# X W of all strips made after the scores, from x1^T kept in att's memory, with VectorE's order in the sort and the fillers moved

## Chip, cores and metric

One core of a Trainium2 chip runs the whole program in one launch. The metric is device time in microseconds (us) of that core. Three runs of the kernel before gave 740.38, 743.62 and 736.76, median 740.38.

## What is computed

N = 2708 nodes with D = 128 features x, and a 0/1 matrix adj (N x N), all float32. Two layers; the change lies where the first ends and the second begins.

```python
# layer 0
deg = clip(adj.sum(1), 1); dis = deg ** -0.5
diffusion = (dis[:, None] * adj * dis[None, :]) @ x - x
attn = softmax(beta * cos_sim(x, x) * adj, axis=1)
x1 = layernorm(x + diffusion + sigmoid(alpha) * (attn @ x - x))
# layer 1
XW = x1 @ W
s_col, s_row = XW @ a[:D], XW @ a[D:]
den = exp(leaky_relu(s_row[:, None] + s_col[None, :], 0.01))
num = adj @ den
att = where(num != 0, den / num, 0)
out = layernorm(x1 + adj @ (att @ XW))
```

## The kernel before

`den` splits into products of exponentials on either side of the bend of leaky_relu. The kernel sorts the nodes by s_row (the k side) and s_col (the j side) into 24 groups of at most 126, and for each group needs one gathered block of rows of adj^T and one of X W. Rows are held in 22 blocks of 128; columns of adj^T in 6 strips of 512 (the last of 148).

**Attention** (up to about 215 us): `att` [128 x 22 x 128] collects the attention term of all blocks. It lies in the pool `lp`, which is closed at L950, before the sort.

**Diffusion** (L865 to L946). For each strip, 22 matmuls `dif_acc` (each written as two instructions), turning, the layer norm into `x1`, turning of x1 (`x1_ps`), and `x1_in_sbuf` (L807), which copies x1^T to `x1_t`. From it come two rows of scores (`scores`, L815: `row` with k = 1 and `col` with k = 0), tallies of how many scores lie below each of 256 thresholds (`tally`, L666), `shared_row` (L832, on ScalarE), and `picked` (L823, scores by node: `sr_p`, `sc_p`). `limited` and `e2` (L839 to L846) make `low` and exp of it, `e2_p`, and put it into `e2_w`. Then `projected` (L848) makes four blocks of X W on TensorE, VectorE copies them to `xw`, and `store_xw` (L857) stores them to the tensor `xw_d` in HBM on ScalarE's queue. Strips 0 to 3 do all this in a loop that Tile orders; strips 4 and 5 (`s` and `t`, from L894) follow in an order that is written out by hand: while `strict` is set, the helpers `mm`, `dve`, `act` and `gps` (L181 to L201) pin each instruction behind the last one of its engine. All their instructions carry the lines of these helpers in the profile (L176 to L201).

**Fillers.** One more sum over all rows of adj^T, weighted by `e2_w`, is kept in two PSUM banks (`tot`). Its work is cut in 22 jobs "e" (`first_strips`, L691: loads a 768 KB row block into `nat`, a pool of three buffers, and 4 matmuls, each two instructions) and 22 jobs "k" (`kept_strips`, L707: 6 matmuls from strips 3, 4 and 5, which are in SBUF). The first nine e jobs load on GpSimd's queue during the diffusion. The rest are placed by hand: `fill("eke")` issues three jobs at that point of TensorE's order; their loads go on SyncE's queue, each waiting for its buffer.

**The look-up of intervals' ends** (`reached`, L737; L984 to L996). From the tallies a table `reach_b` [128 x 256] says where an interval that begins at each threshold ends. Eleven steps on VectorE follow it, each needing the one before (L988): `ends[g] = reach_b[ends[g-1]]`. The result `both` goes through two rounds of matmuls (`ends_ps`, `thr_ps`) to the thresholds `thr`.

**The sort** (L968 to L1242). VectorE: `k_gt`, `k_hot`, a scan `k_run`, `k_own` (which needs `ahead` from TensorE), `k_at`, `k_onp`; then the same for j. ScalarE writes `k_ons` and `j_ons` block by block (`valued`). TensorE makes tables from `onp` and `ons` (`table`, L1101), with fillers between a table and the choice of its rows (`k_sel`). `k_no` (L1116) holds row numbers: with it GpSimd gathers 126 rows of adj^T into `ring` (four buffers; ring 0 is `x_sb`'s memory, the others lie where the strips were), and with `j_no` rows of `xw_d` into `xws`.

**The main loop** (L1340): 24 groups through `num`, `q` and `m_acc`; then the output matmuls.

Pools are stacks at both ends of SBUF. `tab` and `tmp` (L963, L965) are opened at the right end after `lp`, `work2` and `nat` of the diffusion were closed or as they become free, so their tiles lie over old tiles. With `reuse_waits="tile"` the first write to a new tile waits for every reader and writer of each old tile that it overlaps, DMAs among them.

Of the kernel before, what the change touches and what calls it, by code (L numbers as in the profile page):

```python
# [9 lines left out]
F32 = mybir.dt.float32  # L10
AF = mybir.ActivationFunctionType
ALU = mybir.AluOpType
# [33 lines left out]
def grouped(  # L46
# [16 lines left out]
    def pool(name, bufs=1, space=None, side="left", stack=ctx):  # L63
        kw = {"space": space} if space else {}
        return stack.enter_context(
            tc.tile_pool(name=name, bufs=bufs, side=side, reuse_waits="tile", **kw)
        )
# [7 lines left out]
    def blocks(s):  # L75
        return min(SW // P, NB - s * (SW // P))
# [110 lines left out]
    def dve(op, *args, **kwargs):  # L187
        if strict:
            return pinned("DVE", getattr(nc.vector, op), *args, **kwargs)
        return getattr(nc.vector, op)(*args, **kwargs)  # L190

    def act(op, *args, **kwargs):
        if strict:
            return pinned("ACT", getattr(nc.scalar, op), *args, **kwargs)
        return getattr(nc.scalar, op)(*args, **kwargs)  # L195
# [450 lines left out]
    strip_a = pool("strip_a", stack=l0)  # L646
    strip_b = pool("strip_b", stack=l0)
    strip_c = pool("strip_c", stack=l0)
    nat = pool("nat", 3, stack=l0)
    work2 = pool("work2", 2, stack=es)  # L650
    tots = ExitStack()
    ps_tot = pool("ps_tot", 1, PSUM, side="right", stack=tots)
# [63 lines left out]
    def fill(pattern):  # L716

        for c in pattern:
            f, kb = jobs[c].pop(0)
            f(kb, nc.sync)  # L720
# [84 lines left out]
        return tp  # L805

    def x1_in_sbuf(s, tp):  # L807
        nb = blocks(s)
        x1_t = work2.tile([P, SW], F32, tag="x1_t", name="x1_t")
        dve(  # L810
            "tensor_copy", x1_t[:, : nb * P], tp[:, :nb, :].rearrange("p b i -> p (b i)")
        )
        return x1_t

    def scores(s, x1_t, k, pb):  # L815
# [7 lines left out]
    def picked(s, pb, dst):  # L823
        for b in range(blocks(s)):
            ib = s * 4 + b
            junk = work2.tile([P, P], F32, tag="picked", name="picked", bufs=2)
            dve(
                "scalar_tensor_tensor", junk, pb[:, ts(b, P)], 1.0, ident, ALU.mult,
                ALU.mult, accum_out=dst[:, ib : ib + 1],
            )  # L830

    def shared_row(s, pb):  # L832
        n = blocks(s) * P
        act(
            "activation", sr_b[:, s * SW : s * SW + n], pb[:, :n], AF.Copy,
            scale=1.0 - LEAK,
        )

    def limited(b0, b1):  # L839
        dve(  # L840
            "tensor_scalar", low[:, b0:b1], sr_p[:, b0:b1], LIMIT, -LIMIT, ALU.min, ALU.max
        )

    def e2(b0, b1):
        act("activation", e2_p[:, b0:b1], low[:, b0:b1], AF.Exp, scale=LEAK)
        nc.gpsimd.tensor_copy(e2_w[:, b0:b1, 1], e2_p[:, b0:b1])  # L846

    def projected(s, x1_t):  # L848
        pn = ps_mm.tile([P, SW // P, D], F32, tag="mm", name="xw_ps")
        for b in range(blocks(s)):  # L850
            mm(
                nc.tensor.matmul, pn[:, b, :], x1_t[:, ts(b, P)], w_sb,
                start=True, stop=True,
            )
        return pn

    def store_xw(s, xw, nb):  # L857
        nc.scalar.dma_start(
            xw_d[s * SW : s * SW + nb * P, :].rearrange("(b p) d -> p b d", p=P), xw
        )  # L860

    def score_bank():
# [2 lines left out]
    for s in range(NS - 2):  # L865
        v, nb = width(s), blocks(s)
        if s > 0:
            load_strip(s + 1)
        acc = ps_acc.tile([P, SW], F32, tag="acc", name="dif_acc")
        diffuse(s, acc)  # L870
        if s == 0:
            attended(*ended)
        h = mixed(s, turned(to_sbuf(acc, v, nb), nb, ps_tp))
        to_x1(s, h, *moments(h, nb))
        x1_t = x1_in_sbuf(s, x1_turned(s))
        pbs = []
        for k in (1, 0):
            pb = scores(s, x1_t, k, score_bank())
            tally(s, pb, k)
            pbs.append(pb)  # L880
        shared_row(s, pbs[0])
        picked(s, pbs[0], sr_p)
        picked(s, pbs[1], sc_p)
        limited(s * 4, s * 4 + nb)
        e2(s * 4, s * 4 + nb)
        xw = work2.tile([P, 4, D], F32, tag="xw", name="xw")
        nc.vector.tensor_copy(xw, projected(s, x1_t))
        store_xw(s, xw, nb)

        for kb in {1: (0, 1, 2), 2: (3, 4, 5), 3: (6, 7, 8)}.get(s, ()):  # L890
            first_strips(kb, nc.gpsimd)
# [18 lines left out]
    tally(s, row_s, 1, (0,))  # L910
    h_t = mixed(t, rows)
    mv_t = moments(h_t, blocks(t))
    shared_row(s, row_s)
    fill("eke")
    tally(s, row_s, 1, (1,))
    to_x1(t, h_t, *mv_t)
    tp = x1_turned(t)
# [12 lines left out]
    far = small.tile([P, 2], F32, tag="far", name="far")  # L930
    dve("tensor_scalar", far, ct[:, 2:4], G + 0.5, None, ALU.add)
    shared_row(t, row_t)
    picked(t, col_t, sc_p)
    picked(t, row_t, sr_p)
    picked(s, row_s, sr_p)
    fill("ek")
    reach_ps, can = reached(ct_ps)
    limited(s * 4, NB)
    picked(s, col_s, sc_p)
    act("activation", reach_b[64:], can[64:], AF.Copy, scale=-1.0, bias=Q + 1.0)  # L940
    dve("tensor_copy", reach_b[:64], reach_ps[:64, :Q])
    e2(s * 4, NB)
    xw = nat.tile([P, 6, D], F32, tag="xw_last", name="xw", bufs=1)
    act("copy", xw[:, :4, :], projected(s, x1_s))
    act("copy", xw[:, 4:, :], projected(t, x1_t)[:, :2, :])
    store_xw(s, xw, 6)  # L946
    fill("ekekek")
    es.close()
    pss.close()
    lps.close()  # L950
# [14 lines left out]
    tmp = pool("tmp", side="right", stack=sort)  # L965
    ps_x = pool("ps_x", 2, PSUM, stack=sort)

    vk = tmp.tile([P, NB], F32, name="vk")  # L968
    dve("scalar_tensor_tensor", vk, sr_p, -1.0, pad, ALU.mult, ALU.add)
    vj = tmp.tile([P, NB], F32, name="vj")  # L970
    dve("tensor_tensor", vj, sc_p, pad, ALU.add)
    back = tab.tile([P, NB], F32, name="back")
    dve("tensor_tensor", back, live, e2_p, ALU.mult)


    ons = {}
# [8 lines left out]
    ends = tmp.tile([P, half_g], F32, name="ends")  # L985
    dve("tensor_copy", ends[:64, 0:1], reach_b[:64, 0:1])
    dve("tensor_copy", ends[64:, 0:1], reach_b[64:, Q - 1 :])
    for g in range(1, half_g):  # L988
        junk = tmp.tile([P, Q], F32, tag="more", name="junk")
        dve(  # L990
            "scalar_tensor_tensor", junk, bound_no, ends[:, g - 1 : g], reach_b,
            ALU.is_equal, ALU.mult, accum_out=ends[:, g : g + 1],
        )
    both = tmp.tile([P, NG - 1], F32, name="both")
    dve("tensor_scalar", both[:, : half_g - 1], ends[:, : half_g - 1], row0, None, ALU.mult)
    dve("tensor_scalar", both[:, half_g - 1 :], ends, half_on, None, ALU.mult)  # L996
    ends_ps = ps_x.tile([P, SW], F32, tag="ahead", name="ends_ps", bufs=2)
    mm(nc.tensor.matmul, ends_ps[:, : NG - 1], ones, both, start=True, stop=True)
    thr_ps = ps_x.tile([P, SW], F32, tag="x", name="thr_ps", bufs=2)
    fill("k")  # L1000
    for h in range(2):
# [5 lines left out]
        mm(  # L1007
            nc.tensor.matmul, thr_ps[:, : NG - 1], ones, hit, start=(h == 0), stop=(h == 1)
        )
    fill("ekekk")  # L1010
    thr = tmp.tile([P, NG + 1], F32, name="thr")
    gps("memset", thr[:, 0:1], -1e9)
    gps("memset", thr[:, NG:], 100.0)
# [19 lines left out]
    def numbered(name, hot):  # L1033

        run = tmp.tile([P, NG, NB], F32, tag=name + "_gt", name=name + "_run")
        dve(
            "tensor_tensor_scan",
            run.rearrange("p g b -> p (g b)"), going.rearrange("p g b -> p (g b)"),
            hot.rearrange("p g b -> p (g b)"), 0.0, ALU.mult, ALU.add,
        )  # L1040
        of = tab.tile([P, NG], F32, name=name + "_of")
        dve("tensor_copy", of, run[:, :, NB - 1])
        ahead = ps_x.tile([P, SW], F32, tag="ahead", name="ahead", bufs=2)
        mm(nc.tensor.matmul, ahead[:, :NG], after, of, start=True, stop=True)
        return run, ahead, of
# [54 lines left out]

    def table(name, onp, v, o, p0, between):  # L1101

        t = tmp.tile([P, 1, P], F32, name=f"{name}_t{v}")
        partial_table(name, onp, v, o)
        act("copy", t[:, 0, :], o)
        between()
        return selected(name, t, [v], p0)

    def banks(*tags):
        return [  # L1110
            ps_x.tile([P, SW], F32, tag=tag, name="tab_ps", bufs=2)[:, :P] for tag in tags
        ]
# [26 lines left out]
            oob_is_err=False,  # L1139
        )  # L1140


    cs_p = tmp.tile([P, NB], F32, name="cs_p")
    dve("tensor_scalar", cs_p, sc_p, LIMIT, -LIMIT, ALU.min, ALU.max)
    dve("tensor_scalar", cs_p, cs_p, 1.0 - LEAK, None, ALU.mult)

    k_gt = beyond("k", vk)
    k_hot = grouped_by("k", k_gt)
    k_run, k_ahead, k_of = numbered("k", k_hot)
    valued("k", 0, k_hot, from_n)  # L1150
    valued("k", 1, k_hot, low, 0, 17)
    fill("kekekekek")
    j_gt = beyond("j", vj)
    k_own = chosen("k", k_hot, k_run, k_ahead)
    k_onp = placed("k", k_own)
    j_hot = grouped_by("j", j_gt)
    k_tab = table("k", k_onp, 0, *banks("x"), P - G, lambda: fill("kk"))
    valued("k", 1, k_hot, low, 17)
    valued("j", 1, j_hot, cs_p, 0, 12)
    j_run, j_ahead, j_of = numbered("j", j_hot)  # L1160
    k_no = rows_of_table("k", k_tab, G)
    valued_by_dve("j", 0, j_hot, from_n)
    k_tab = table("k", k_onp, 1, *banks("x"), 0, lambda: fill("kkk"))
    valued("j", 1, j_hot, cs_p, 12)
    fill("k")
    assert not any(jobs.values()), jobs
    j_own = chosen("j", j_hot, j_run, j_ahead)

# [745 lines left out]
```

## Time and profile before

| what | value |
| --- | --- |
| median of 3 runs | 740.38 us (736.76 to 743.62) |
| the profiled execution: time, span | 739.68 us, 737.9 us |
| TensorE busy in the span | 708.7 us, 96% |
| VectorE, ScalarE, GpSimd busy | 443.8, 419.5, 233.9 us |
| mean granted TensorE clock | 0.982 |
| diffusion | about 217 to 345 us |
| tallies, look-up, sort | about 345 to 395 us |
| main loop from | 395.3 us |

How to read it: times count from the start of the profiled span. PE is TensorE's matmuls and PEld its weight loads, DVE VectorE, ACT ScalarE, POOL GpSimd, SP SyncE; a "q" behind a name means that the engine's queue issued a DMA. In the timeline a row gives start, length, engine, line, operation, tiles written and read, shape and count; at its end, in brackets, the idle time of that engine before it and what ended it. Neighbours of one kind are merged and may overlap others. A view of waits gives who waited for whom, us in total, times, longest.

### The profile page before, as it was taken

To read this page: it belongs to the slowest core of one execution; us is meant where nothing else is said; L and a number is where in the kernel's file an instruction comes from. 1 tells how busy PE (TensorE), PEld (TensorE's weight loads), DVE (VectorE), ACT (ScalarE), POOL (GpSimd) and SP (SyncE) were. 2 spreads that over 40 slices of the span, in tenths; PEclk is the share of its full clock that TensorE was granted. 3 is DMA by queue.
4 is the path that set the end of the run, shared out by engine and by line. 5 is a ranking of instruction groups with operands and counts; after the bars stand their busy time and mean duration, and the time that the engine had idled before them with its cause. 6 is when DMAs were issued, how large, how long until landed. Compare 5 with 4: busy or idle time off the path is not lost. (4 is left out here: it accounts for less than half of the span.)

```text
span 737.9 us, 7958 instructions
## 1 busy us (share of the span) xinstructions
PE 708.7 (96%) x2639; PEld 358.8 (49%) x2639; DVE 443.8 (60%) x925; ACT 419.5 (57%) x601; POOL 233.9 (32%) x240
## 2 busy tenths in 40 slices
PE   7999999999999999999798899999999999999995
PEld 4454444545464444445565344444444446444444
DVE  5676857566541452344787879999999984103032
ACT  4757867778741121211176899999999994001000
POOL 5868788879841000000004222222222300000000
PEclk9999999999979999999989999999999999999999
DMA  8868999988999998731847994444444531999970
GB/s 287 314 226 300 325 326 338 336 316 299 301 365 400 364 395 301 288 143 33 286 143 251 230 222 149 167 173 171 165 158 155 165 133 42 298 311 309 313 228 24
DMA packets 69827, 179.89 MB, mean 244 GB/s; under 512 B 6798, under 2 KB 20914, under 8 KB 66754
## 3 DMA queue, kind: packets, MB, share of 16 engines
q1 hardware_dynamic: 57188, 133.32, 52.4%
q0 software_dynamic: 6336, 43.08, 17.7%
q10 hardware_dynamic: 6254, 2.90, 1.4%
q8 instruction: 23, 0.38, 0.2%
q14 instruction: 26, 0.21, 0.1%
HBM read 176.44 MB, written 2.84 MB: 243 GB/s over the span
## 5 line engine op out<-in xcount | busy, mean ns | idle before, releaser
L201 POOL TENSOR_TENSOR total<-total,p_t 128x512 f32<-128x512 f32 (+3 forms) x111 | 124.5, 1122 | 38.3 <-ACT p_t L195 32.8
L176 PE MATMUL m_acc<-q,xws 128*128 128x512 f32 x240 | 122.2, 597 | 0.0
L176 PE MATMUL num<-ring,wt 128*128 128x512 f32 x216 | 98.8, 550 | 4.4 <-DVE q L176 3.3
L190 DVE SCALAR_TENSOR_TENSOR p_t<-sim,gentle,piece 128x512 f32<-128x512 f32 (+1 forms) x111 | 72.2, 670 | 48.5 <-PE sim L185 37.8
L185 PE MATMUL att_acc<-p_t,x_sb 128*128 128x512 f32 (+1 forms) x228 | 97.6, 555 | 2.0 <-ACT p_t L195 1.8
L185 PE MATMUL dif_acc<-strip,x_sb 128*128 128x512 f32 x220 | 98.4, 594 | 0.0
L195 ACT ACTIVATE p_t<-p_t,shift 128x512 f32<-128x512 f32 (+1 forms) x111 | 69.4, 655 | 35.0 <-DVE p_t L190 29.6
L176 DVE SCALAR_TENSOR_TENSOR q<-sr_b,nc_s,q 128x1536 f32<-128x1536 f32 (+1 forms) x48 | 77.8, 1623 | 17.8 <-ACT q L176 17.6
L176 DVE COPY q<-num 128x512 f32<-128x512 f32 (+1 forms) x142 | 83.9, 612 | 4.4 <-PE num L176 4.2
L176 PEld LDWEIGHTS m_acc<-q,xws 128*128 128x128 f32 x240 | 45.9, 192 | 56.9 <-issue 56.7
L1451 PE MATMUL h_acc<-ring,m_sb 128*128 128x512 f32 x164 | 72.3, 593 | 0.0
L176 ACT ACTIVATE q<-q,head,rest 128x1536 f32<-128x1536 f32 (+1 forms) x48 | 70.2, 1508 | 1.2 <-DVE ring L176 0.9
L176 ACT ACT_TABLE_LOAD x52 | 66.7, 1283 | 3.8 <-issue 2.9
L176 PEld LDWEIGHTS num<-ring,wt 128*128 128x128 f32 x216 | 39.4, 191 | 49.2 <-issue 34.2
L176 ACT ACTIVATE q<-q,c_s 128x1536 f32<-128x1536 f32 (+1 forms) x48 | 62.9, 1355 | 0.4
L185 PEld LDWEIGHTS att_acc<-p_t,x_sb 128*128 128x128 f32 x228 | 40.9, 202 | 45.0 <-ACT p_t L195 25.0
L185 PEld LDWEIGHTS dif_acc<-strip,x_sb 128*128 128x128 f32 x220 | 40.5, 190 | 45.8 <-issue 45.8
L176 ACT ACTIVATE row<-row 128x1354 f32<-128x1354 f32 x44 | 58.2, 1323 | 7.5 <-DMA row<-in_adj 7.5
L1461 ACT COPY ht<-h_acc 128x512 f32<-128x512 f32 (+1 forms) x6 | 3.2, 535 | 91.3 <-PE h_acc L1451 91.2
L1466 DVE TENSOR_TENSOR hh<-rows,x 128x512 f32<-128x512 f32 (+1 forms) x6 | 3.8, 641 | 84.1 <-PE rows L1385 81.7
L176 POOL DMA_INDIRECT ring<-in_adj_t,k_no x18 | 21.1, 1170 | 100.3 <-PE num L176 97.2
L1451 PEld LDWEIGHTS h_acc<-ring,m_sb 128*128 128x128 f32 x164 | 30.8, 190 | 36.8 <-issue 36.8
(289 smaller groups left out, 907.8 us busy)
## 6 DMA issues: line engine op xcount, KB each, us to landing
row<-in_adj SPq DMA_DIRECT2D x44, 677.0 KB, 5.4
strip<-in_adj_t SPq DMA_DIRECT2D x10, 2816.0 KB, 19.3
piece<-in_adj_t SPq DMA_DIRECT2D x24, 1024.0 KB, 7.0
ring<-in_adj_t SPq DMA_DIRECT2D x20, 1024.0 KB, 5.0
nat<-in_adj_t SPq DMA_DIRECT2D x13, 768.0 KB, 4.5
x_sb<-in_adj_t SPq DMA_DIRECT2D x7, 1024.0 KB, 5.0
nat<-in_adj_t POOLq DMA_DIRECT2D x9, 768.0 KB, 9.8
piece<-in_adj_t SPq DMA_DIRECT2D x7, 512.0 KB, 6.6
```

The source lines that it names most:

```text
L176: latest[engine] = op(*args, **kwargs)
L185: op(*args, **kwargs)
L190: return getattr(nc.vector, op)(*args, **kwargs)
L195: return getattr(nc.scalar, op)(*args, **kwargs)
L201: getattr(nc.gpsimd, op)(*args, **kwargs)
L1451: nc.tensor.matmul(acc[:, : h1 - h0], m_sb[:, kb + b, :], a[:, b, h0:h1], start=(kb + b == 0), stop=(kb + b == NB - 1),)
L1461: nc.scalar.copy(ht[:, h0:h1], acc[:, : h1 - h0])
L1466: nc.vector.tensor_tensor(hh[:, b0 : b0 + n, :], rows[:, :n, :], x1[:, ib + b0 : ib + b0 + n, :], ALU.add)
```

## The change

- Every strip's x1^T is written over that strip's part of `att` instead of a tile of `work2`. `mixed` has read the part before.
- `projected`, its copy and its store leave the loop of strips 0 to 3 and the end of strips 4 and 5. `project(n)` makes X W of strip n from att and ScalarE copies it back to att. All six stand behind `reached`, with `limited` and `e2` after the third. Two stores replace five: strips 0 to 2 (768 KB) and 3 to 5 (640 KB).
- `nat` has four buffers.
- `shared_row(s, row_s)` comes after that of t; `reach_b`'s ScalarE part comes before the projections.
- In the sort, `vk`, `vj` and `cs_p` come after `both`, `back` after the hits; `j_ons` for table 0 comes ahead of `k_no`.
- The look-ups' scratch tile is x_sb's memory. `tmp` first takes a tile with the tag `onp`; the two k tables share one tile.
- Fillers are spread anew: 1 e and 3 k fewer ahead of the look-up's end, and as many more behind.

```diff
-    nat = pool("nat", 3, stack=l0)
+    nat = pool("nat", 4, stack=l0)
...
     def x1_in_sbuf(s, tp):
         nb = blocks(s)
-        x1_t = work2.tile([P, SW], F32, tag="x1_t", name="x1_t")
-        dve(
-            "tensor_copy", x1_t[:, : nb * P], tp[:, :nb, :].rearrange("p b i -> p (b i)")
-        )
+        x1_t = att[:, s * 4 : s * 4 + nb, :].rearrange("p b i -> p (b i)")
+        dve("tensor_copy", x1_t, tp[:, :nb, :].rearrange("p b i -> p (b i)"))
         return x1_t
...
-    def projected(s, x1_t):
+    def project(s):
+        mine = att[:, s * 4 : s * 4 + blocks(s), :]
         pn = ps_mm.tile([P, SW // P, D], F32, tag="mm", name="xw_ps")
         for b in range(blocks(s)):
             mm(
-                nc.tensor.matmul, pn[:, b, :], x1_t[:, ts(b, P)], w_sb,
-                start=True, stop=True,
-            )
-        return pn
-
-    def store_xw(s, xw, nb):
+                nc.tensor.matmul, pn[:, b, :], mine[:, b, :], w_sb, start=True, stop=True
+            )
+        act("copy", mine, pn[:, : blocks(s), :])
+
+    def store_xw(s0, s1):
+        b0, b1 = s0 * 4, min(s1 * 4, NB)
         nc.scalar.dma_start(
-            xw_d[s * SW : s * SW + nb * P, :].rearrange("(b p) d -> p b d", p=P), xw
+            xw_d[b0 * P : b1 * P, :].rearrange("(b p) d -> p b d", p=P), att[:, b0:b1, :]
         )
...
         e2(s * 4, s * 4 + nb)
-        xw = work2.tile([P, 4, D], F32, tag="xw", name="xw")
-        nc.vector.tensor_copy(xw, projected(s, x1_t))
-        store_xw(s, xw, nb)
...
-    shared_row(s, row_s)
-    fill("eke")
+    fill("eeke")
...
     shared_row(t, row_t)
+    shared_row(s, row_s)
...
     reach_ps, can = reached(ct_ps)
-    limited(s * 4, NB)
+    act("activation", reach_b[64:], can[64:], AF.Copy, scale=-1.0, bias=Q + 1.0)
     picked(s, col_s, sc_p)
-    act("activation", reach_b[64:], can[64:], AF.Copy, scale=-1.0, bias=Q + 1.0)
     dve("tensor_copy", reach_b[:64], reach_ps[:64, :Q])
-    e2(s * 4, NB)
-    xw = nat.tile([P, 6, D], F32, tag="xw_last", name="xw", bufs=1)
-    act("copy", xw[:, :4, :], projected(s, x1_s))
-    act("copy", xw[:, 4:, :], projected(t, x1_t)[:, :2, :])
-    store_xw(s, xw, 6)
-    fill("ekekek")
+
+    for n in range(NS):
+        project(n)
+        if n == 2:
+            store_xw(0, 3)
+            limited(s * 4, NB)
+            e2(s * 4, NB)
+    store_xw(3, NS)
+    fill("e")
...
-    vk = tmp.tile([P, NB], F32, name="vk")
-    dve("scalar_tensor_tensor", vk, sr_p, -1.0, pad, ALU.mult, ALU.add)
-    vj = tmp.tile([P, NB], F32, name="vj")
-    dve("tensor_tensor", vj, sc_p, pad, ALU.add)
-    back = tab.tile([P, NB], F32, name="back")
-    dve("tensor_tensor", back, live, e2_p, ALU.mult)
+    tmp.tile([P, NB, P], F32, tag="onp", name="onp")
...
+    junk = x_sb.rearrange("p b d -> p (b d)")[:, :Q]
     for g in range(1, half_g):
-        junk = tmp.tile([P, Q], F32, tag="more", name="junk")
...
     dve("tensor_scalar", both[:, half_g - 1 :], ends, half_on, None, ALU.mult)
+    vk = tmp.tile([P, NB], F32, name="vk")
+    dve("scalar_tensor_tensor", vk, sr_p, -1.0, pad, ALU.mult, ALU.add)
+    vj = tmp.tile([P, NB], F32, name="vj")
+    dve("tensor_tensor", vj, sc_p, pad, ALU.add)
+
+    cs_p = tmp.tile([P, NB], F32, name="cs_p")
+    dve("tensor_scalar", cs_p, sc_p, LIMIT, -LIMIT, ALU.min, ALU.max)
+    dve("tensor_scalar", cs_p, cs_p, 1.0 - LEAK, None, ALU.mult)
...
-    fill("ekekk")
+    fill("ekekek")
+    back = tab.tile([P, NB], F32, name="back")
+    dve("tensor_tensor", back, live, e2_p, ALU.mult)
...
-        t = tmp.tile([P, 1, P], F32, name=f"{name}_t{v}")
+        t = tmp.tile([P, 1, P], F32, tag=name + "_t", name=name + "_t")
...
-    cs_p = tmp.tile([P, NB], F32, name="cs_p")
-    dve("tensor_scalar", cs_p, sc_p, LIMIT, -LIMIT, ALU.min, ALU.max)
-    dve("tensor_scalar", cs_p, cs_p, 1.0 - LEAK, None, ALU.mult)
...
-    fill("kekekekek")
+    fill("kkekkekke")
...
-    k_tab = table("k", k_onp, 0, *banks("x"), P - G, lambda: fill("kk"))
+    k_tab = table("k", k_onp, 0, *banks("x"), P - G, lambda: fill("k"))
...
+    valued_by_dve("j", 0, j_hot, from_n)
     k_no = rows_of_table("k", k_tab, G)
-    valued_by_dve("j", 0, j_hot, from_n)
-    k_tab = table("k", k_onp, 1, *banks("x"), 0, lambda: fill("kkk"))
+    k_tab = table("k", k_onp, 1, *banks("x"), 0, lambda: fill("kekk"))
     valued("j", 1, j_hot, cs_p, 12)
-    fill("k")
+    fill("kkkk")
```

## The prediction

> **What bounds the kernel now.** I read the page, then the timeline of TensorE from 225 to 345 us, the timeline of all engines from 340 to 400, the waits of VectorE and TensorE from 355 to 396, the DMA issues with their landings, and busy time by stretch. On the page TensorE is busy 96% of the span, which says little of the stages. Two stages matter.
>
> In the diffusion TensorE never stands still. Timeline, TensorE alone (start, length, what):
>
> ```profile
> 296.85 3.60 PE L185 MATMUL dif_acc<-strip,x_sb 128*128 128x512 f32 x8
> 300.29 1.05 PE L185 MATMUL xw_ps<-w_sb,x_t 128*128 128x128 f32 x8
> 301.18 10.46 PE L185 MATMUL dif_acc<-strip,x_sb 128*128 128x512 f32 x24
> ```
>
> Four blocks of X W cost 301.18 - 300.29 = 0.89 us of issue, and there is no gap before or after: in this stage every TensorE instruction counts.
>
> Then comes the look-up of intervals' ends, where VectorE alone carries the end. Timeline, all engines:
>
> ```profile
> 357.87 1.50 PE L176 MATMUL xw_ps<-w_sb,x_t 128*128 128x128 f32 x12
> ...
> 358.07 0.38 ACT L176 ACTIVATE reach_b<-can_ps 64x256 f32<-64x256 f32 x1 [5.09 <-PE can_ps L176]
> ...
> 358.47 1.28 ACT L176 ACT_TABLE_LOAD   x1
> ...
> 360.00 0.86 ACT L176 COPY xw<-xw_ps 128x512 f32<-128x512 f32 x2
> 360.00 0.18 DVE L176 TENSOR_TENSOR back<-live,e_p 128x22 f32<-128x22 f32 x1 [1.52 <-ACT e_p L176]
> 360.10 0.30 DVE L176 COPY ends<-reach_b 64x1 f32<-64x1 f32 x2
> ...
> 360.88 0.36 ACTq L858 DMA_DIRECT2D xw_d<-xw  x1
> ...
> 366.65 0.59 PE L176 MATMUL ends_ps<-both,ones 128*128 128x23 f32 x2 [3.71 <-DVE both L176]
> ```
>
> VectorE loses 1.52 us on `e_p` before the chain of 11 look-ups begins at 360.10; TensorE stands 3.71 us. Busy time by stretch (PE, PEld, DVE, ACT, POOL, then the granted clock):
>
> ```profile
> 358.30:366.65 8.35, 4.64 (x70) 3.19 (x69) 6.28 (x30) 2.50 (x5) 0.93 (x5) 0.96 0.77 250
> 366.65:372.83 6.18, 6.18 (x47) 3.86 (x51) 3.81 (x11) 1.41 (x6) 0.00 (x0) 0.50 0.57 193
> ```
>
> After the pause TensorE runs at half clock for 6.2 us. Later waits of VectorE on the way to the main loop (us, times, longest):
>
> ```profile
> DVE k_no L176 <- PE k_sel L176: 1.3, 1, 1.3
> DVE k_run L176 <- PE ahead L176: 0.8, 1, 0.8
> ```
>
> From 401 us ACT is the bound (8.85 us a group, no gaps but one).
>
> **What the skill says.** "TensorE: Matmul & The Clock Gate", What's actually happening: the array's clock halves after an idle window of about 3.4 us and the window runs freely; the trace agrees (half clock after the 3.71 us pause). "DMA: Bandwidth & Descriptors", Anatomy of one DMA: a DMA has a fixed part, mostly completion, and its semaphore moves only after the last byte is confirmed. Same page, Queues, rings and completion order: an engine takes its queues in turn, packet by packet. The trace agrees with both: the store of X W landed thus (KB, us to landing), first with nearly nothing beside it, then beside three row loads:
>
> ```profile
> xw_d<-xw ACTq DMA_DIRECT2D x1, 256.0 KB, 2.3
> ```
> ```profile
> xw_d<-xw ACTq DMA_DIRECT2D x1, 384.0 KB, 8.3
> ```
>
> **The change part by part.** All times are on the axis of before.
>
> 1. X W leaves the diffusion: 4 strips x 0.89 = -3.56 us, since TensorE has no gap there. With it go 4 VectorE copies (0.69 each) and 4 stores, all hidden; nothing for them. The fourth row buffer lets one more 768 KB load start at 223 us. The strips' loads have slack: that of strip 2's second half lands at 263.49 and is wanted 11 x 0.86 us after that.
>
> 2. ACT's row of strip 4 moves behind the tallies: VectorE's 0.84 us wait on `sr_b` at 348.58 goes; VectorE is busy without a break from there to 358.2, so reach and can come 0.75 earlier: can_ps ends near 357.3.
>
> 3. The new wait. In the order of the built program the first copy to `ends` waits for ACT's last copy of X W and for two DMA semaphores, and their counts are those of both stores of xw_d. The reason is the memory: the tile `onp`, now taken first, fills the low end of the pool, so that `ends` and what follows lie where att was (att at bytes 171808 to 183072, `ends` at 176384); att now holds X W until both stores have read it. In before, `ends` waited only for an old store. So the look-up is not beside the projections but after them. Its start:
>  - TensorE: 8 products per strip in 0.89 us; two banks, so strip n waits for the copy of n-2. ACT: a 128x512 copy 0.58, table load 1.28, exponent 0.21, DMA issue 0.37.
>  - Copies 0, 1, 2 end at 358.8, 359.7, 360.6; load and exponent to 362.2; first store (768 KB) issued at 362.2; copies 3, 4 end at 363.2, 363.7; strip 5's products wait for copy 3, its copy ends at 364.2; second store (640 KB) issued at 364.2.
>  - A 64 KB store late in the kernel lands in 1.57, the 256 KB one in 2.30: 192 KB in 0.73, 263 KB/us, and 1.33 fixed. Both stores: 362.2 + 1.33 + 1408/263 (5.35) = 368.9, if alone. Beside them runs one row load, issued when the one `e` filler is done, at about 364.2: 768 KB at the 420 GB/s that busy stretches show, 1.9 us on the same engines. If it wins each turn: 370.8. In before the store landed near the end of its neighbours, so I take 370.4; ends of the range 368.5 and 372.
>  So `ends` starts at 370.4 instead of 360.1: +10.3 us. Queued behind it on VectorE is the whole sort, and behind that the main loop. GpSimd's j_ons memset waits for the same stores, with thr's memsets behind it; they are wanted 9 us later.
>
> 4. From `ends` to the thresholds: 11 look-ups, unchanged. vk, vj and cs_p hide in the 0.78 us wait for ends_ps; cs_p out of the way of k_gt: -0.3. TensorE has now stood some 12 us, so this part is at half clock as before. `ekekek` has one e more than `ekekk`, about +0.9 at that clock: `ahead` comes +0.5 net. After it there are no row waits (before 0.97 and 0.15), TensorE is ready when k_onp is, and the k table starts at the same distance from `ends` (20.8 us). `back`: 0.18 in the wait for thr.
>
> 5. j_ons ahead of k_no on VectorE (1.14 us in the 1.3 us wait), and one k filler fewer ahead of k_sel: j_run -0.5. But `kekk` and `kkkk` hold 4 fillers more (e 0.5, k 0.62), so the j table starts +0.7; with no pause it runs at full clock, 2.9 us instead of 4.5: main loop -0.9. If half clock remains there it is +0.7. The memory of ring 1 comes free with the last filler, 2.2 us later; its gather took 9.1 us behind gather 0 and 7.4 alone, so it lands about +0.6, before group 1 wants it. Then ACT's one gap in the ramp is the wait for `wt` from g_d (2.65 us), which hangs on DMA that is full from 400 us: the 0.9 will be partly given back; I take -0.4 (from -0.9 to +0.7).
>
> Sum: -3.56 + 10.3 - 0.4 = +6.3 us. Against the profiled execution (span 737.9, time 739.68): 746.0. The median of the runs, 740.38, is 0.7 above that execution: 746.5.
>
> **Rivals.**
>  - *Stores worse than costed.* The row load takes its turns and some of the 16 engines end late, as in before (384 KB in 8.3 us, with a thin tail): `ends` at 372.5 to 374, total +8.5 to +10, 749 to 751. For it: the 8.3. Against: three loads ran then, one now.
>  - *The look-up does run beside the projections* (other side). It would if the memory under `ends` were free when reach_b is. Then `ends` starts at 357.75 (-2.35), TensorE's projections end near 364.2 as ends_ps is due at 364.3, no half clock (-1.2 to the thresholds, -0.8 at `ahead`), cs_p -0.3, tail -1.0: -5.7, and with the diffusion -9.3: 731. Against: the wait counts in the program. It decides below 364.1, where 10.3 - 6.3 is used up; the second store cannot even be issued before 364.2.
>  - *The change of order gives nothing in the diffusion*: something else fills TensorE's 0.89 us (a strip late by the extra row load). Then +9.8, 750. Against: the landings above.
>  - *A cheap wait*: stores land at 368.5 and the loop keeps -0.9: +4.0, 744.
>
> **How the numbers follow.** Forecast with its cheap variant 0.65 (743 to 749), stores worse 0.18, diffusion gives nothing 0.06, beside the projections 0.11. The range 741 to 751 leaves out the 731 case (0.11) and what lies beyond the slow ones' costing (about 0.06). 1% is 7.4 us, about what a measurement of this kernel can tell from no change; +6.3 lies just inside. About 0.2 of the forecast's 0.65 passes +7.4, or 0.13, and nearly all of the slow cases: slower 0.35; faster 0.10; within 1% 0.55.
>
> **What the profile after would show.** Right: no xw_ps between dif_acc, strips 0.9 us closer; VectorE idle some 12 us before `ends`, put down to the DMA of xw_d or to ACT; TensorE idle 11 us or more before ends_ps; both stores landing 6 to 8 us after the first issue; j table without half clock. Wrong if VectorE goes from `low` to `ends` with no wait, or if the stores land under 5 us after the first issue, or if TensorE waits for strips in the diffusion.

## The result, and the profile after

The changed kernel takes 745.64 us (median of 14 runs, 743.03 to 749.06) against 738.14 for the kernel before (14 runs on the same chips, 734.91 to 745.96): ratio 1.0090, 95% interval 1.0067 to 1.0112. It is 0.9% slower. The ratio is that of the fast runs and stands for 6.6 us (4.9 to 8.3), while the two medians as they are lie 7.5 us apart. Forecast were 746.5, 741 to 751. The profiled execution of after took 746.63 us, span 744.9.

The diffusion is as forecast. Timeline of the kernel after, TensorE alone (start, length, engine, line, what): no `xw_ps` stands between the matmuls of `dif_acc`.

```profile
298.98 13.04 PE L185 MATMUL dif_acc<-strip,x_sb 128*128 128x512 f32 x30
311.94 0.85 PE L185 MATMUL tot<-nat,e_w 128*32 128x384 f32 x6
```

So is the new wait. Timeline of the kernel after, all engines; in brackets the idle time before the row and what ended it:

```profile
355.99 0.60 PE L176 MATMUL can_ps<-fits,ones 128*128 128x256 f32 x2
...
356.43 4.72 PE L176 MATMUL xw_ps<-w_sb,att 128*128 128x128 f32 x40
356.63 0.38 ACT L176 ACTIVATE reach_b<-can_ps 64x256 f32<-64x256 f32 x1 [4.59 <-PE can_ps L176]
...
359.96 1.28 ACT L176 ACT_TABLE_LOAD   x1
359.97 0.39 ACTq L858 DMA_DIRECT2D xw_d<-att  x1
...
362.63 0.85 PE L176 MATMUL tot<-nat,e_w 128*32 128x384 f32 x8
...
363.14 0.38 ACTq L858 DMA_DIRECT2D xw_d<-att  x1
363.54 0.33 SPq L693 DMA_DIRECT2D nat<-in_adj_t  x1
369.30 0.31 DVE L176 COPY ends<-reach_b 64x1 f32<-64x1 f32 x2 [12.43 <-DMA xw_d<-att]
369.31 0.39 POOL L974 MEMSET j_ons<- 128x352 f32 x1 [7.27 <-DMA xw_d<-att]
```

`reach_b` is complete at 357.01, and nothing that `ends` computes with is missing from there on. Yet VectorE stands until 369.30, and the view names the DMA of X W as what ended the wait. GpSimd's memset of `j_ons`, which overlies att too, is let go 0.01 us later. The landing of the second store itself is not in this trace. What this does to TensorE shows in busy time by stretch (PE, PEld, DVE, ACT, POOL, then granted clock, DMA share, GB/s):

```profile
356.59:369.30 12.71, 6.05 (x53) 5.05 (x51) 0.28 (x3) 4.96 (x9) 0.52 (x2) 0.81 0.70 234
369.30:375.76 6.46, 0.00 (x1) 0.00 (x1) 6.05 (x28) 0.00 (x0) 0.47 (x3) 0.50 0.00 0
375.76:381.57 5.81, 5.81 (x46) 3.87 (x50) 3.85 (x12) 1.05 (x5) 0.00 (x0) 0.50 0.13 20
```

In the second row VectorE works nearly alone: TensorE and the DMA engines do nothing, since the look-up's result is what all else needs. In the third TensorE works at half clock. Of VectorE's waits after `ends`, the one of `k_no` for `k_sel` (1.3 us in before) is gone; up to 405 us these of over 1 us remain (that of `j_t` for its table was 2.5 in before):

```profile
DVE ends L176 <- DMA xw_d<-att: 12.4, 1, 12.4
DVE j_t L176 <- PE tab_ps L176: 1.6, 1, 1.6
DVE thr L176 <- PE thr_ps L176: 1.5, 1, 1.5
DVE k_run L176 <- PE ahead L176: 1.4, 1, 1.4
```

The whole can be cut at four events of the timeline: first `dif_acc`, last `can_ps` (end), first `ends`, first `num`. In us, with two more executions of each kernel that are told below:

| execution | attention: start to dif_acc | dif_acc to can_ps | can_ps to ends | ends to num | num to end |
| --- | --- | --- | --- | --- | --- |
| before | 217.35 | 140.69 | 2.07 | 35.22 | 342.56 |
| before, 2nd | 219.87 | 140.69 | 2.07 | 35.23 | 340.87 |
| before, 3rd | 218.74 | 140.67 | 2.07 | 34.35 | 347.99 |
| after | 220.40 | 136.19 | 12.70 | 33.25 | 342.38 |
| after, 2nd | 220.85 | 136.19 | 12.69 | 34.57 | 344.71 |
| after, 3rd | 219.73 | 136.20 | 12.79 | 34.93 | 342.83 |

The two columns that hold the forecast's large terms repeat within 0.1 us: -4.49 and +10.66. The third that the change touches has -0.68 in the mean (34.25 for 34.93), but its single executions spread by 0.9 us in before and by 1.7 in after. Together they make +5.5 us.

### The profile page after: what moved, and what is told of

Its sections match the earlier page's. It is cut to its first block, busy times and chain, and to the rows that moved or that the text cites. A ratio compares the mean times of both kernels' runs of the same rounds, so it can differ in the third digit from the quotient of the medians.

```text
span 744.9 us, 7943 instructions
## 1 busy us (share of the span) xinstructions
PE 710.0 (95%) x2639; PEld 358.1 (48%) x2639; DVE 440.9 (59%) x921; ACT 421.7 (57%) x605; POOL 233.2 (31%) x240
## 5 line engine op out<-in xcount | busy, mean ns | idle before, releaser
L185 PE MATMUL att_acc<-p_t,x_sb 128*128 128x512 f32 (+1 forms) x228 | 99.3, 563 | 3.5 <-ACT p_t L195 3.1
```

What stands on the lines that cost most here:

```text
L185: op(*args, **kwargs)
```

## Experiments

All ratios are to the kernel before, timed on the same chip; intervals are 95%.

**1. `ends` off att.** One line of the changed kernel goes:

```diff
-    tmp.tile([P, NB, P], F32, tag="onp", name="onp")
```

> The changed kernel with one line less: the tile onp is no longer taken first in its pool, so that ends and the small tiles after it do not lie on the memory of att; the first to wait for the two stores of xw_d is then the compare j_gt, much later. Theory of the wait (the one in the prediction): ends starts about 2 us after the end of can_ps, as in the kernel before, beside the projections; TensorE does not stand idle for 12 us and is not granted half clock there; of the 10.65 us that the trace of the changed kernel shows there all comes back, and what is left is the gain of the other parts (4.5 us in the diffusion, 2 us in the sort): 731 to 735 us, 0.985 to 0.996 of the kernel before. Rival (the projections themselves are in the way: TensorE, ACT and VectorE do the look-up and X W in turn, or j_gt takes over the wait): ends starts early, but hit or k_gt comes late by the same amount, and the time stays at or above that of the kernel before, 738 to 746 us.

Measured: 730.69 us, ratio 0.9886 (0.9848 to 0.9924). Timeline, all engines:

```profile
353.57 0.38 ACT L176 ACTIVATE reach_b<-can_ps 64x256 f32<-64x256 f32 x1 [4.60 <-PE can_ps L176]
...
353.76 0.37 DVE L176 COPY ends<-reach_b 64x1 f32<-64x1 f32 x2
...
360.07 0.38 ACTq L858 DMA_DIRECT2D xw_d<-att  x1
```

Busy time by stretch, same columns as above:

```profile
353.53:360.35 6.82, 5.99 (x54) 5.05 (x52) 6.35 (x31) 4.96 (x9) 1.21 (x5) 1.00 0.63 218
360.35:381.95 21.60, 19.73 (x378) 15.32 (x378) 19.26 (x27) 16.19 (x70) 1.15 (x1) 1.00 0.65 233
```

The same projections, copies and stores now run under the look-up: TensorE 5.99, VectorE 6.35 and ScalarE 4.96 us busy in the same 6.82 us, where the changed kernel did them in 12.71 + 6.46. `ends` begins 0.23 us after can_ps, and the clock stays full. So the work of X W is not in the way; one tile's address is. The rival falls. The wait for the stores doesn't vanish, it moves to `j_gt`, the next tile that lies on att; there VectorE stands 1.1 us, which hardly reaches further (from the first copy to `thr` to the second `k_run` 5.14 us, before 4.97).

**2. The second store taken away from the wait.**

```diff
-    store_xw(3, NS)
+    nc.scalar.dma_start(
+        xw_d[12 * P :, :].rearrange("(b p) d -> p b d", p=P), x_sb[:, 12:NB, :]
+    )
```

The rows of strips 3 to 5 in xw_d then come from x_sb: the kernel leaves their X W out.

> The changed kernel with the second store of xw_d (strips 3 to 5) taken from x_sb and not from att: rows 12 to 21 of xw_d then hold other numbers, and ends waits for one store and for the last copy of X W. Theory of the wait: ends starts when the first store has landed, about 364 us in the trace of the changed kernel in place of 369.3, and the time falls by about 5 us against the changed kernel, to 740 us or 1.002 of the kernel before. Rival (stores do not set the start; the projections do): ends starts no earlier than 367 and the time stays at 745.

Measured: 741.18 us, 1.0022 (1.0000 to 1.0044). Timeline:

```profile
359.36 0.38 ACTq L858 DMA_DIRECT2D xw_d<-att  x1
364.24 0.31 DVE L176 COPY ends<-reach_b 64x1 f32<-64x1 f32 x2 [7.98 <-DMA xw_d<-att]
```

`ends` starts 8.26 us after can_ps instead of 12.70: 4.4 us earlier, and the ratio is 0.0068 lower, 5.0 us. The rival falls.

**3. One store more.** Its edit doubles `store_xw(3, NS)`.

> The changed kernel with the second store of xw_d given twice, one after the other (the repeat waits until the first has landed, as it writes the same rows); nothing computed differs. Theory of the wait: ends starts later by the whole time of one more store, 4.1 to 6 us, and the time rises by as much, to 750 to 752 us, ratio 1.015 to 1.018. Rival (the wait at ends has slack behind it, since the sort later waits for something else anyway): the time rises by less than 2 us.

Measured: 750.06 us, 1.0141 (1.0096 to 1.0187). Timeline, where the first row is the second and third issue merged, and then the page's row of DMA issues (KB, median us to landing):

```profile
358.31 6.67 ACTq L858 DMA_DIRECT2D xw_d<-att  x2
358.71 0.33 SPq L693 DMA_DIRECT2D nat<-in_adj_t  x1
368.43 0.31 DVE L176 COPY ends<-reach_b 64x1 f32<-64x1 f32 x2 [16.39 <-DMA xw_d<-att]
```

```profile
xw_d<-att ACTq DMA_DIRECT2D x2, 640.0 KB, 4.9
```

`ends` starts 16.66 us after can_ps, 4.0 later than in the changed kernel, and the ratio is 0.0051 higher, 3.8 us. The time of a store is paid in full: in the trace -4.4 for one fewer to wait for and +4.0 for one more (4.1 to 6 were expected), in the ratios -5.0 and +3.8. The two 640 KB stores tell more: the second landed 6.23 us after its issue, with the row load beside it, the third in 3.63 alone (median of the two 4.9).

**4. The order alone, in the kernel before** (`shared_row` and `limited` later; vk, vj, cs_p behind `both`; `back` behind the hits; `j_ons` ahead of k_no):

```diff
-    shared_row(s, row_s)
...
     shared_row(t, row_t)
+    shared_row(s, row_s)
...
-    back = tab.tile([P, NB], F32, name="back")
-    dve("tensor_tensor", back, live, e2_p, ALU.mult)
...
+    back = tab.tile([P, NB], F32, name="back")
+    dve("tensor_tensor", back, live, e2_p, ALU.mult)
```

> The kernel before with VectorE's order alone changed (shared_row and limited later, vk, vj and cs_p behind both, back behind the hits, the j table's ones ahead of k_no); X W, its stores and the row buffers as before. Theory of the prediction: the wait for the picked row of the last strip goes (0.84 us), back and cs_p leave the way (0.75 and 0.3 us) and k_no does not hold the j table: 2 to 3.5 us less, 735 to 736 us, ratio 0.995 to 0.997. Rival (the sort's end hangs on ACT and on the rows from HBM and not on VectorE's order): ACT waits longer for wt from g_d, and the time stays within 0.2% of the kernel before.

Measured: 736.19 us, 0.9955 (0.9929 to 0.9981). Against the mean of the three executions of before, dif_acc to can_ps takes 139.73 (-0.96), can_ps to ends 0.23 (-1.84), ends to num 33.39 (-1.5). The rival's 0.2% lies at the very edge of the interval, so by the times it all but falls. The wait of `wt` for g_d, 1.4 us here, can't decide: in before it took from 0.7 to 9.3 us (experiment 9).

**5. The move alone**: the kernel of experiment 1 with that order undone, its diff the reverse of the last one.

> The kernel in which ends lies off att, with VectorE's order of the kernel before put back (shared_row, limited, e2, vk, vj and back ahead of ends; cs_p and k_no where they were): X W made at the end from att and the fillers and row buffers of the change are all that is left of it. Theory: the move out of the diffusion gives its 3.56 us, and the order gives the rest; of the 8.8 us by which the kernel off att beats the one before, the order alone was worth 3.3, so this one stays about 3 us above the kernel off att: 733 to 735 us, ratio 0.991 to 0.994, with the wait of VectorE for sr_b back and ends 2 us after can_ps. Rival (the order matters only where X W is in the strips): within 1 us of the kernel off att, 730 to 731.5.

Measured: 734.82 us, 0.9927 (0.9900 to 0.9954). dif_acc to can_ps takes 137.12, that is -3.57. Its timeline has both waits back:

```profile
345.25 0.75 DVE L176 TENSOR_SCALAR_CACHE_REDUCE junk<-sb_ps,ntheta 128x512 f32<-128x512 f32 x1 [0.85 <-ACT sr_b L176]
...
356.68 0.18 DVE L176 TENSOR_TENSOR back<-live,e_p 128x22 f32<-128x22 f32 x1 [1.52 <-ACT e_p L176]
356.78 0.30 DVE L176 COPY ends<-reach_b 64x1 f32<-64x1 f32 x2
```

The product of the two ratios, 0.9955 x 0.9927 = 0.9882, is that of experiment 1, 0.9886: move and order add up once the wait is away.

**6. Three row buffers** in the kernel of experiment 1.

```diff
-    nat = pool("nat", 4, stack=l0)
+    nat = pool("nat", 3, stack=l0)
```

> The kernel in which ends lies off att, with three row buffers in place of four. Theory of the prediction: the row loads in this stretch hide behind TensorE's work, and the fourth buffer is worth next to nothing: within 1 us of the kernel off att, 730 to 732 us. Rival (three rows hold up the row sums, the fillers of TensorE stall on nat, TensorE idles and loses clock): 1.5 to 4 us slower, 732.5 to 735, with waits of tot for nat and half clock in the sort.

Measured: 732.73 us, 0.9895 (0.9857 to 0.9933). The sign that the rival named is there, waits of TensorE for rows (0.6 us in experiment 1), but the stretch from dif_acc to the end takes 511.37 us, with four buffers 511.32:

```profile
PE tot L176 <- DMA nat<-in_adj_t: 2.8, 4, 1.6
```

So the fourth buffer is worth nothing that the trace shows. The two medians, 2.0 us apart, were timed on different chips; the ratios leave 0.7 us between them, far inside their intervals. In the traces the difference lies in attention (219.54 against 217.33), before the first load into `nat`. This run also shows what holds `j_gt`. The view names ScalarE:

```profile
368.74 0.73 DVE L176 TENSOR_TENSOR j_gt<-vj,thr 128x550 f32<-128x550 f32 x1 [1.15 <-ACT k_ons L176]
```

But the second store, issued at 362.29, took 6.33 us and landed at 368.62, 0.12 us before `j_gt` starts: it is the store.

**7. The old fillers** in the kernel of experiment 1.

```diff
-    fill("e")
+    fill("ekekek")
...
-    fill("ekekek")
+    fill("ekekk")
```

(and before's patterns at the five other places.)

> The kernel in which ends lies off att, with the fillers of the kernel before (fewer k ahead of the tables, more behind them). Theory of the prediction: fillers are work that has to be done somewhere, and moving them among idle places costs 0 to 1 us: 730 to 732 us. Rival (the new spread keeps TensorE from idling where X W left, and the old spread puts a filler ahead of a product that the look-up needs): 1 to 3 us slower, 732 to 734.

Measured: 736.75 us, 0.9941 (0.9918 to 0.9963). More than either theory gave. Timeline of TensorE:

```profile
362.34 0.85 PE L176 MATMUL tot<-nat,e_w 128*32 128x384 f32 x8
363.01 0.68 PE L176 MATMUL tot<-strip,e_w 128*32 128x293 f32 x12
...
365.29 0.69 PE L176 MATMUL tot<-strip,e_w 128*32 128x293 f32 x12
365.91 0.40 PE L176 MATMUL ends_ps<-both,ones 128*128 128x23 f32 x2
```

Six fillers stand ahead of `ends_ps` in TensorE's order, and VectorE waits for it:

```profile
DVE hit L176 <- PE ends_ps L176: 2.9, 1, 2.9
DVE j_gt L176 <- DMA xw_d<-att: 2.4, 1, 2.4
```

In before the same six were done in time, and TensorE still stood 3.71 us after them; six strips of X W now take up that pause. ends to ends_ps takes 9.38 us (6.59 in experiment 1). Five row loads are issued while the second store is under way; it takes 10.4 us, so `j_gt` waits another 2.4. ends to num is 35.70, with the new spread 32.84: the spread is worth 2.9 us in the traces, 4.1 by the ratios. The old spread was not run in the changed kernel itself. TensorE is idle 12.3 us there, and six fillers take some 3.6 (362.34 to 365.9 above), so an estimate from these numbers is that it would cost little there.

**8. Three row buffers in the changed kernel.**

> The changed kernel with three row buffers in place of four; ends still waits for both stores. In the changed kernel a row load was issued 0.4 us after the second store, and the store took 6.1 us to land where the first had taken 4.1. Theory of contention (the row load shares the engines with the store and lengthens the wait): if the load comes at another time the store lands up to 2 us earlier, and the time is up to 2 us lower, 743.5 to 745. Rival (the store is slow for its own 640 KB and not for the row load, or three rows put a load there just the same): ends starts 12.5 to 13 us after can_ps, and the time stays within 0.5 us of the changed kernel, or rises by what the fourth buffer is worth.

Measured: 747.44 us, 1.0104 (1.0066 to 1.0141); `ends` 13.08 us after can_ps. It doesn't settle contention: a row load is still issued 0.4 us after the second store, which took 6.4 us. The pair of stores in experiment 3 does.

**9. Each kernel profiled twice more**, unchanged.

> The kernel before, profiled once more, to see what one profiled execution is worth. Theory (chance of an execution): what differs from execution to execution is the attention stage, whose end has lain between 214.9 and 220.4 us with one and the same list of instructions, by how long half clock was granted there; from the first dif_acc to the end the kernel before takes 520.5 us again, within 1 us. Rival (the one trace of before was a good execution in its later part, which is why the traces show 4.0 us there where the medians show 6.6): 517 or 523.

> The kernel before, profiled a third time: as for the second. Theory 520.5 us from the first dif_acc to the end, within 1 us; rival 517 or 523.

> The changed kernel, profiled once more. Theory: ends starts 12 to 13 us after can_ps again, and from the first dif_acc to the end it takes 524.5 us, within 1 us. Rival (the later part varies by itself): off by 2 us or more, with another row of half clock in the sort.

> The changed kernel, profiled a third time: as for the second. Theory 524.5 us from the first dif_acc to the end, within 1 us, and an attention stage that ends anywhere between 214 and 221 us; rival off by 2 us or more.

Measured, first dif_acc to the end: before 518.86 and 525.08 (520.54 the first time), after 528.17 and 526.74 (524.52). The theory, within 1 us, fails in all four: they are off by 1.7 to 4.5 us. The rival has it nearer: the later part varies by itself. What the change touches repeats to 0.1 us up to `ends`, but the last stretch of one kernel spreads over 7 us. The third execution of before shows one place, in the waits of all engines after 395 us:

```profile
ACT wt L176 <- DMA wt<-g_d: 9.3, 1, 9.3
```

That one wait for a row from HBM took 2.6, 0.7 and 9.3 us in before, 1.3, 3.8 and 1.9 in after. The means over three executions differ by 1.7 us in attention, +5.5 from dif_acc to num and -0.5 after it, in all 6.7; the ratio of the runs gives 6.6. Attention runs the same instructions in both kernels, so its 1.7 us is no step of the change that these runs show; that it is mere chance isn't shown either, with three executions a side that lie between 217.4 and 220.9.

## Why the prediction was right

The forecast named one mechanism, a wait made by where a tile lies in memory, and it decided the sign. The level alone, 745.64 for 746.5, would say less: before itself came out at 738.14 in the 14 runs, not at the 740.38 that the forecast started from. The test is the difference, +6.6 us for +6.3, and in the traces +5.5 of it lie where the change works, up to the first `num`. Point by point:

- **X W out of the diffusion, -3.56.** Measured -3.57 (experiment 5) and -3.54 (changed kernel against experiment 4). Four gaps of 0.89 on an engine that never stands add without loss.
- **The wait on `sr_b`, -0.75.** Measured -0.96 in experiment 4 and -0.92 between experiments 5 and 1; nothing of it was given back.
- **The new wait, `ends` 13.1 us after can_ps (370.4 - 357.3).** Measured 12.70. That the path was right is shown by experiments 1 to 3; that its length came out so well is in part luck. The table load and the exponent were put ahead of the first store, which in fact is issued at 359.97, with the load: 3.4 us after can_ps, not 4.9. `ends` hangs on the second store, issued 6.55 after can_ps (forecast 6.9), and lets go within 6.2 us of that, as forecast (364.2 to 370.4). But the forecast made these 6.2 of 4.7 for the store alone, since it had the bytes of the first still ahead (368.9 - 364.2), and 1.5 for the row load. The runs show 3.6 alone and 2.5 to 2.8 more with one row load: two errors of about 1.1 us that cancel. For the same reason the sign "both stores landing 6 to 8 us after the first issue" was missed: `ends` starts 9.3 us after it. The Trainium skill ("DMA: Bandwidth & Descriptors", Queues, rings and completion order) says that a DMA engine drains a packet of one queue and goes on to the next. No packet's turn is shown here; the traces agree in that neighbours cost time, if in no plain proportion: 640 KB took 3.6 us alone, 6.2 to 6.4 with one 768 KB row load issued while it ran, 6.3 with three, and 10.4 with five.
- **From `ends` on, -0.4.** Not settled. Up to the first `num` the mean is -0.68, less than the 1.7 us by which three executions of after spread; the first trace alone (-1.97) would have called this term five times too small. From `ends` to the end the mean is -1.2, and three executions of before spread by 6.2 us there. Of its parts, the k table starts 20.7 to 21.5 us after `ends` (before 20.8 to 21.4), as forecast. The j table runs at full clock in all three executions of after, in 2.81, 3.33 and 3.32 us (forecast 2.9). In before it took 4.48 twice, partly at half clock, but 3.00 at full clock the third time, so this gain hangs on the execution. The forecast gave back half in the wait for `wt`; that wait varies by 8.6 us from one execution to the next, so a give-back of 0.5 can neither be seen nor denied.
- **Fillers.** Their spread entered the sum only as small shifts; in the changed kernel no run tests that. What the prediction did not see is that it is a needed part of the move: without the wait, the old spread costs 2.9 us in the traces.
- **The rival of the other side.** "Look-up beside the projections, if the memory under `ends` were free, 731" was turned down by reading which semaphores `ends` waits for. Experiment 1 frees that memory: 730.7. Its sum holds: -9.3 forecast, -8.8 measured in the medians. In the trace its terms up to `ends` give -6.3 (forecast -5.9) and those from there to the first `num` -2.1 (forecast -3.3 with the tail).

So the kernel is slower because one wait outweighs gains of some 8 to 9 us that are real: against experiment 1, `ends` comes 12.5 us later after can_ps (12.70 for 0.23), and ends to num takes 1.4 more, with TensorE at half clock. The best version of all that ran is the changed kernel without its first tile in `tmp`, ratio 0.9886 to before.

## What to carry to other kernels

When a tile gets a longer life, look up what will be allocated over its memory next and who writes that first: here a tile that was taken first in its pool, long before it was written, pushed a tile of 12 columns onto a buffer that a DMA still read, and the critical chain waited for a store to HBM. Cost such a wait as issue, fixed part, bytes, and whatever load shares the engines, and check each of these terms, since errors in them can cancel. And when work moves into a pause, the fillers ahead of the pause must move behind it.

## What the runs showed of the hardware

- One and the same list of instructions, the attention stage, took 214.9 to 220.9 us. It goes with how long half clock was granted in it: none, 214.88 (experiment 8); 3.4 us, 215.57 (experiment 3); 10.2 to 13.7 us in the other executions, 217.3 to 220.9. That is not all of it: with the same 10.2 us it took from 217.33 (experiment 1) to 219.87 (before, second execution). What brings half clock there, no run shows.
- Half clock needs no whole window of rest. The mean clock of 0.81 over the 12.71 us to 369.30 means that half clock began some 4.8 us before their end, near 364.5 (12.71 x 0.19 / 0.5); the last TensorE instruction there ended at 363.48 (362.63 + 0.85, in the timeline above), about 1 us earlier. So the idle window of about 3.4 us ahead of half clock, which the prediction cites and finds in before, is not borne out by the trace of after.
- Half clock outlasts the pause. In after TensorE works again from 375.76, and full clock returns at 381.57, 5.81 us later; in before 6.2 us after the pause (366.65 to 372.83). The Trainium skill ("TensorE: Matmul & The Clock Gate", What's actually happening) has full clock return after at least one busy window of some 3.4 us; the trace agrees with "at least", with nearly two.
- A view of waits can name another releaser than the last. At `j_gt` in experiment 6 it named ScalarE, though a store had landed 0.12 us before; the landing of each DMA, where the trace has it, tells the two apart.
